# GpSimd in the text's order, scatters one a turn, shared rows behind the last count, and more buffers for the routed tiles

## The chip, the cores and the metric

The kernel runs on one core of a Trainium2 chip. The metric is the device time of one execution in microseconds (us). Its engines are called as in the profile: PE (matrix products; PEld is its weight load), DVE (vector), ACT (activations), POOL (GpSimd) and SP (which issues most DMAs). Each engine takes its instructions in the order in which they were put down, and an instruction that waits holds all that stand behind it on that engine. L12 is line 12 of the kernel before.

## The reference, cut to what matters

Four layers follow each other on x, of shape (4, 512, 128), each a cross attention to a context of 77 tokens and a feed-forward part:

```python
x = x + L0_xattn(ctx, ctx, layernorm(x));   x = x + L0_ffn(layernorm(x))
x = x + L1_xattn(layernorm(x), ctx, ctx);   x = x + L1_ffn(layernorm(x))
x = x + L2_xattn(layernorm(x), ctx, ctx);   x = x + L2_ffn(layernorm(x))
x = x + L3_xattn(layernorm(x), ctx, mask);  x = x + L3_ffn(layernorm(x))
```

Three of the feed-forward parts are mixtures of eight experts. The first sends each token to its two best experts, weighted, and adds a shared expert that sees all tokens:

```python
gates = sigmoid(xf @ Wg);  vals, idx = top_k(gates, 2);  vals = vals / vals.sum(-1)
w = zeros.at[arange(T)[:, None], idx].add(vals)
shared = silu(xf @ Ws1) * (xf @ Ws3) @ Ws2
h = silu(einsum('td,edf->tef', xf, We1)) * einsum('td,edf->tef', xf, We3)
out = (shared + einsum('tef,efd,te->td', h, We2, w)) / 3
```

The second sends each token to one expert, up to a capacity of 320 tokens per expert, with one hidden layer of 512; the fourth sends each token to one expert without a capacity. The third feed-forward part is dense.

## The kernel before

The 2048 tokens are worked on in four rows of 512 (the batch entries, b = 0 to 3). A row is 128 partitions by NT = 4 blocks of 128 features.

**Routing.** After a row's first attention, `route0` (L1064) normalises it: statistics `mv` on DVE, `std` and `rstd` on POOL (L192, L194), the result `xr` on DVE (L199). It transposes it (L207), copies it to `hT` (L213), forms the gates (L1027, L1036), and picks two experts per token on DVE. `Router.count` (L922, last product L943) counts on PE how many earlier tokens go to each expert, so each token has a place `to` (L1106) in a buffer `xbuf` in DRAM. `Router.send` (L956) then scatters the rows there with indirect DMAs that POOL issues (L958): four for the first choice, then a copy of `xr` on POOL (L1099), then four for the second. After the last row `Router.tiles` (L975) forms on DVE a table `tab` of the buffer positions and experts of the tiles (256 places of one expert each), and `far`, which marks empty places. The second layer's `route1` (L1296) copies the tokens beside the normalised rows on POOL (`xw`, L1300) and has four scatters a row. The last layer's goes as the first's, with four.

**Routed tiles.** The first feed-forward part (from here: the first stage, 217 to 322 us) has 23 tiles. `tile_rows` (L1041) lets SP read a position and an expert from `tab` and issue two loads: the rows `xt` (L1046, three buffers) and the expert's weights `wt` (L1049, four buffers). `layer1` (L1248 on) transposes the rows on PE, copies them to `hTt` on ACT, takes the tokens' numbers `idx` on DVE (L1252) and their weights `wgt` (L1254), both in three buffers, and `gated` (L1213) forms the hidden layer in two halves: products L1218 and L1219 on PE, silu on ACT (L1221), product `hid` on DVE (L1222). `layer2` multiplies by the second weights (L1262), scales to `ye` on ACT (L1268, three buffers), and `give_rows` (L1052) scatters `ye` to the tokens' places in `ybuf` by two indirect DMAs on POOL (L1053). A buffer of `idx` or `ye` is free again when its scatter has read it. The second part (middle stage, 471 to 526 us) has eight tiles, one per expert; the last (1021 to 1114 us) has 15 tiles with products L1370 and L1381, `idx` at L1744, and `ye` at L1754 on DVE, scattered to the output.

**The shared expert and the next constants.** `shared(b)` (L1226) uses `gated` on a whole row (L1218, L1219, L1221, L1222), multiplies by the second weights (L1231) and adds to x on DVE (L1236). Rows 0 and 1 stand in the text ahead of the tiles, rows 2 and 3 behind them. `PlainCross` (L1110) forms the keys and values of the second attention from the context: a product L1117, and `values3` (L235), which fills three tiles with zeros on POOL (L240) and has twelve products L245 whose results DVE adds a bias to and spreads out (L248, L257).

**What sets the order.** Outside of the attentions a scheduler puts each engine's instructions in the order of its own costs; it may move an instruction ahead of others of the text as far as its data allow. Inside `attend` (L505) the order of the text is kept for the engines of ORDERED (L501: PE, DVE and ACT), not for POOL, and what stands behind in the text may be placed between them by the scheduler. There the text itself interleaves generators: `side` is the list of those that are open, `turn` (L481) steps the one that is due, a `yield` ends its turn, and `yield -1` asks for the next turn. When the main sequence is over, `round_of_turns` steps each in turn, with two warming products between rounds (`warm`, L166, a product of constants whose result nobody reads).

Of the kernel before, what the change touches and what calls it, by code (L numbers as in the profile page):

```python
# [8 lines left out]
F32 = mybir.dt.float32  # L9
BF16 = mybir.dt.bfloat16  # L10
U8 = mybir.dt.uint8
I32 = mybir.dt.int32  # L12
# [47 lines left out]
def tile_kernel(ctx: ExitStack, tc: tile.TileContext, ins, out):  # L60
# [438 lines left out]
                side_step(gen)  # L499

    ORDERED = {getattr(mybir.EngineType, e) for e in ("PE", "DVE", "Activation")}  # L501

    def attend(units, lead, turns, fill=8):

# [37 lines left out]
                if begun and (u < 3 or ends[u - 3] - 1 <= n):  # L542
                    launch(u)

        with tc.manual_schedule(engines=ORDERED):
            pairs = 0
            launch(0)
            while starts[0] in side:
                warm(fill)
                side_step(starts[0])  # L550
                turn()
            for n in range(-lead, len(seq) + 1):
                un = old = None
                if 0 <= n < len(seq):
                    u, i = seq[n]
                    if i == 0:
                        side_drain(readies[u])
                    if i < units[u].shape.steps:
                        un = units[u]
                if 0 < n:  # L560
                    v, j = seq[n - 1]
                    if j < units[v].shape.steps:
                        old = units[v]
                        if j == 0 and old.late is not None:
                            if v not in lates:
                                lates[v] = old.late(old)
                                side_add(lates[v])
                            side_drain(lates[v])
                whole = n + lead >= len(seq)
                if whole:  # L570
                    banks[:] = [3]
                for k in range(2):
                    if un is not None and (k == 0 or not whole):
                        sc = []
                        for c in (0, 1) if whole else (k,):
                            sc.append(un.scores_t(i, c, whole and pairs % 3 == 2))
                            pairs += whole
# [336 lines left out]
    class Router:  # L914
# [7 lines left out]
        def count(self, b, oh):  # L922
# [17 lines left out]
                    pp[:, :n], lhsT=onesb, rhs=runb.rearrange("p i e -> p (i e)"), start=False, stop=False  # L940
                )
            for i in range(1, NT):
                nc.tensor.matmul(  # L943
                    pp[:, i * E : n], lhsT=onesb, rhs=of[:, : (NT - i) * E], start=False, stop=i == NT - 1
                )
            return pp[:, :n].rearrange("p (i e) -> p i e", e=E)
# [8 lines left out]

        def send(self, rows, to):  # L956
            for i in range(NT):
                d = nc.gpsimd.indirect_dma_start(  # L958
                    out=self.xbuf, out_offset=bass.IndirectOffsetOnAxis(ap=to[:, i : i + 1], axis=0),
                    in_=rows[:, i, :], in_offset=None, bounds_check=self.xbuf.shape[0] - 1, oob_is_err=False,  # L960
                )
                apart(d, self.sent)
                self.sent.append(d)
# [76 lines left out]

    def tile_rows(pool, tab, xbuf, w, t, width, wcols, sent):  # L1041

        xt = pool.tile([128, 2 * width], F32, tag="xt", name="xt", bufs=3)
        at = nc.sync.value_load(tab[0:1, 0, t : t + 1], min_val=0, max_val=xbuf.shape[0] - TS)
        src = xbuf[bass.ds(at, TS), :].rearrange("(p two) d -> p (two d)", two=2)
        after_all(nc.sync.dma_start(out=xt, in_=src), sent)  # L1046
        wt = pool.tile([128, wcols], F32, tag="wt", name="wt", bufs=4)
        e = nc.sync.value_load(tab[0:1, 1, t : t + 1], min_val=0, max_val=(E - 1) * 128)
        nc.sync.dma_start(out=wt, in_=w[bass.ds(e, 128), :])  # L1049
        return xt.rearrange("p (i d) -> p i d", i=2), wt  # L1050
# [14 lines left out]
    def route0(b):  # L1065
# [28 lines left out]
        for k, (oh, m) in enumerate(((oh1, m1), (oh2, m2))):  # L1094
# [9 lines left out]
            slot = router0.pick(at, oh, "slot")  # L1104
            to = small.tile([128, NT], I32, tag="to", name="to")
            nc.vector.tensor_scalar(to, slot, -1.0, None, ALU.add)  # L1106
            router0.send(rows, to)


    class PlainCross:  # L1110
# [95 lines left out]

    mid, ahead = ExitStack(), ExitStack()
    ap1 = ahead.enter_context(tc.tile_pool(name="ahead", bufs=2))
    plain = PlainCross(ap1, NK, p2, p2("kb"), p1("bv1"))
    with tc.tile_pool(name="moe0", bufs=2) as mpool:  # L1210
        tab, far = router0.tiles(N0)

# [22 lines left out]
            xf = xs[b].rearrange("p i d -> p (i d)")  # L1235
            nc.vector.scalar_tensor_tensor(xf, py, 1.0 / 3.0, xf, ALU.mult, ALU.add)  # L1236

        for b in range(2):
            shared(b)
        warm(16)  # L1240
        given = []
        first = {}

        def layer1(t):
# [3 lines left out]
                nc.tensor.transpose(ps[:, i * 128 : (i + 1) * 128], xt[:, i, :D], ident)  # L1248
            hT = mpool.tile([128, TS], F32, tag="hTt", name="hTt")
            nc.scalar.copy(hT, ps[:, :TS])  # L1250
            idx = mpool.tile([128, 2], I32, tag="idx", name="idx", bufs=3)
            nc.vector.tensor_tensor(idx, xt[:, :, 129], far[:, t, :], ALU.max)  # L1252
            wgt = mpool.tile([128, 2], F32, tag="wgt", name="wgt", bufs=3)
            nc.vector.tensor_copy(wgt, xt[:, :, 128])  # L1254
            first[t] = gated(hT, w[:, 0:256], w[:, 256:512], TS), w, idx, wgt

        def layer2(t):
            hid, w, idx, wgt = first.pop(t)
            py = mm_tile()
            for i in range(2):  # L1260
                for c in range(2):
# [1 line left out]
                        py[:, i * 128 : (i + 1) * 128], lhsT=hid[:, c, i * 128 : (i + 1) * 128],  # L1263
                        rhs=w[:, 512 + c * 128 : 640 + c * 128], start=c == 0, stop=c == 1,
                    )
            ye = mpool.tile([128, 2, D], F32, tag="ye", name="ye", bufs=3)
            for i in range(2):
                nc.scalar.mul(ye[:, i, :], py[:, i * 128 : (i + 1) * 128], wgt[:, i : i + 1])  # L1268
            for i in range(2):
# [27 lines left out]
    def route1(b):  # L1297
# [23 lines left out]
        nc.vector.tensor_tensor(far, far, pos, ALU.add)  # L1321
        to = small.tile([128, NT], I32, tag="to", name="to")
        nc.vector.tensor_tensor(to, far, first, ALU.add)
        router1.send(xr, to)

    def finish1(b, o_tok):
        yield from project_add(o_tok, 1, p2("wo"), xs[b])
# [60 lines left out]
    with tc.tile_pool(name="moe1", bufs=2) as mpool:  # L1388
# [10 lines left out]
        def layer1(e):  # L1399
# [11 lines left out]
                nc.tensor.transpose(ps[:, o : o + n], xe[:n, i, :D], ident[:n, :n])  # L1411
            hT = mpool.tile([128, CAP], F32, tag="hTe", name="hTe")
            nc.scalar.copy(hT, ps[:, :CAP])
            idx = mpool.tile([128, 3], I32, tag="idx", name="idx", bufs=3)
            nc.vector.tensor_tensor(idx[:, 0:2], xe[:, 0:2, 257], far1[:, e, 0:2], ALU.max)
            nc.vector.tensor_tensor(idx[:64, 2:3], xe[:64, 2, 257:258], far1[:64, e, 2:3], ALU.max)
            held[e] = xe, idx, relu_layer1(mpool, hT, p3("w1")[:, e * 512 :], p3("b1")[:, e * 4 :], CAP)
# [1 line left out]
        def layer2(e):  # L1419
# [2 lines left out]
            pt = mm_tile()  # L1422
            for i, (o, n) in enumerate(cuts):
                nc.tensor.transpose(pt[:n, i * D : (i + 1) * D], yT[:, o : o + n], ident)
            ye = mpool.tile([128, 3, D], F32, tag="ye", name="ye", bufs=3)
# [26 lines left out]
    def route3(b):  # L1452
# [17 lines left out]
        router3.send(xr, to)  # L1470


    ys = {}
# [256 lines left out]
    with tc.tile_pool(name="moe3", bufs=2) as mpool:  # L1730
# [5 lines left out]
        def layer1(t):  # L1736
# [6 lines left out]
            idx = mpool.tile([128, 2], I32, tag="idx", name="idx", bufs=3)  # L1743
            nc.vector.tensor_tensor(idx, xt[:, :, 256], far[:, t, :], ALU.max)  # L1744
            held[t] = xt, w, idx, relu_layer1(mpool, hT, w, w[:, 1024:1028], TS)

        def layer2(t):
# [5 lines left out]
            ye = mpool.tile([128, 2, D], F32, tag="ye", name="ye", bufs=3)  # L1753
            nc.vector.tensor_tensor(  # L1754
                ye, pt[:, :TS].rearrange("p (i d) -> p i d", i=2), xt[:, :, D : 2 * D], ALU.add
            )
# [136 lines left out]
```

## Time and profile before

| | us |
|---|---|
| median of 3 runs | 1118.06 (1117.11 to 1126.39) |
| the profiled execution | 1115.88 |
| its span, first to last instruction | 1114.0 |
| busy: PE / DVE / ACT / POOL | 913.8 / 551.7 / 428.6 / 293.4 |
| first attention and routing | 0 to 217 |
| first stage of routed tiles | 217 to 322 |
| second attention and routing | 338 to 470 |
| middle stage (eight experts) | 471 to 526 |
| third and fourth attention, dense part | 528 to 1016 |
| last stage of routed tiles | 1021 to 1114 |

The mean granted clock of PE is 0.886 of full speed. A row of a timeline gives the start, the duration, the engine, the line, what it made of what, and in brackets how long the engine had stood idle before it and what ended that. A row of waits gives who waited, for what, how long in total, how often, and the longest. "SPq" is the queue of DMA issues on SP. Not every instruction has its record in the trace (a few per cent are missing).

### The profile page before, as it was taken

Reading aid. Unit: us, or ns where it says so; the run is one execution under the profiler, and the core shown is the slowest. Engines: PE = TensorE matmul, PEld = TensorE weight load, DVE = VectorE, ACT = ScalarE, POOL = GpSimd, SP = SyncE. Lnnn points to the kernel's source line nnn. Section 1 sums busy time; section 2 is a strip of 40 time slices with the busy share of each in tenths; the row PEclk is TensorE's granted clock in tenths of the full one; section 3 lists DMA queues with packets and bytes.
Section 4 is the critical chain, followed back from the end, with each engine's and each line's share of the span. In section 5 each row is a group of like instructions: output and inputs, shape, how many; then the busy total and the mean of one; then the engine's idle time right before and its main releaser. Section 6 shows DMA issues by size and latency. Waiting matters only on the chain. (4 is left out here: it accounts for less than half of the span.)

```text
span 1114.0 us, 15855 instructions
## 1 busy us (share of the span) xinstructions
PE 913.8 (82%) x5602; PEld 448.8 (40%) x5602; DVE 551.7 (50%) x1733; ACT 428.6 (38%) x647; POOL 293.4 (26%) x350
## 2 busy tenths in 40 slices
PE   5898876587878987696699888888899999983885
PEld 2444433376753434254355234332222232331764
DVE  3455334422235655232655325468787888813232
ACT  1164332133421544032232143334565666760332
POOL 4010334234431222335422002324003101012233
PEclk8999688889997997699688589999899999996999
DMA  9999200155433000121200000773516200002552
GB/s 301 283 272 294 62 20 19 45 167 152 144 101 152 10 26 23 31 79 40 54 4 10 1 0 6 167 160 83 118 40 150 52 3 21 2 20 68 169 164 85
DMA packets 75393, 100.20 MB, mean 90 GB/s; under 512 B 9143, under 2 KB 63365, under 8 KB 74291
## 3 DMA queue, kind: packets, MB, share of 16 engines
q1 hardware_dynamic: 66915, 88.08, 29.5%
q0 software_dynamic: 5760, 9.33, 2.5%
q10 hardware_dynamic: 2640, 1.79, 0.5%
q8 instruction: 44, 0.72, 0.3%
q14 instruction: 34, 0.28, 0.1%
HBM read 49.69 MB, written 51.13 MB: 90 GB/s over the span
## 5 line engine op out<-in xcount | busy, mean ns | idle before, releaser
L393 ACT ACTIVATE pT<-sc 128x1024 f32<-128x1024 f32 (+5 forms) x198 | 201.3, 1022 | 174.6 <-PE sc L382 108.3
L838 DVE TENSOR_REDUCE mx<-mm 128x1 f32<-128x512 f32 x248 | 156.7, 682 | 38.1 <-PE mm L308 32.3
L407 PE MATMUL mm<-pT,vv 128*32 128x256 f32 (+4 forms) x1216 | 117.3, 454 | 4.6 <-ACT oT L426 3.7
L776 DVE TENSOR_REDUCE mx<-mm 128x4 f32<-128x308 f32 (+1 forms) x120 | 51.7, 472 | 83.9 <-PE mm L312 48.9
L1053 POOL DMA_INDIRECT ybuf<-ye,idx x70 | 67.5, 965 | 93.5 <-ACT ye L1268 50.3
L170 PE MATMUL mm<-steady,onesb 128*128 128x512 bf16 x222 | 66.4, 426 | 12.7 <-DVE vs L1177 1.7
L192 POOL TENSOR_SCALAR std<-mv 128x4 f32<-128x4 f32 x40 | 9.6, 239 | 243.0 <-DVE mv L190 228.1
L958 POOL DMA_INDIRECT xbuf<-xw,to x32 | 32.2, 1006 | 118.7 <-DVE to L1469 60.3
L373 PE MATMUL sc<-q,kbd 32*77 32x512 f32 (+2 forms) x204 | 57.8, 701 | 0.6 <-ACT pT L393 0.6
L213 ACT COPY hT<-mm 128x512 f32<-128x512 f32 x28 | 16.4, 584 | 106.4 <-PE mm L207 106.3
L382 PE MATMUL sc<-qr,kr 32*128 32x512 bf16 x246 | 48.3, 394 | 4.0 <-DMA qr<-mTS 4.0
L308 PE MATMUL mm<-eight 64*128 64x512 bf16 x184 | 44.8, 393 | 7.2 <-DVE mx L838 5.1
L958 POOL DMA_INDIRECT xbuf<-xr,to x32 | 32.1, 1002 | 57.2 <-DMA xbuf<-zero 18.3
L776 DVE TENSOR_REDUCE mx<-sc 128x8 f32<-128x616 f32 (+1 forms) x36 | 27.3, 797 | 39.0 <-PE sc L329 28.8
L407 PEld LDWEIGHTS mm<-pT,vv 128*32 128x32 f32 (+3 forms) x1216 | 26.5, 109 | 49.1 <-issue 39.4
L1053 POOL DMA_INDIRECT out_dram<-ye,idx x30 | 29.1, 971 | 57.4 <-DVE ye L1754 34.1
L1222 DVE TENSOR_TENSOR hid<-sc,sl 128x256 f32<-128x256 f32 (+1 forms) x54 | 24.7, 462 | 36.5 <-ACT sl L1221 30.3
L1218 PE MATMUL sc<-hTt,wt 128*128 128x256 f32 x92 | 32.4, 438 | 12.6 <-DVE hid L1222 4.4
L194 POOL TENSOR_TENSOR rstd<-std,power 128x4 f32<-128x4 f32 x40 | 41.6, 1041 | 3.3
L170 PEld LDWEIGHTS <-onesb 128*128 128x128 bf16 x222 | 22.2, 105 | 49.3 <-issue 35.1
L1221 ACT ACTIVATE sl<-sc 128x256 f32<-128x256 f32 (+1 forms) x54 | 22.3, 415 | 46.6 <-PE sc L1219 32.5
L382 PEld LDWEIGHTS <-kr 32*128 32x128 bf16 x256 | 11.5, 91 | 70.7 <-issue 70.7
(341 smaller groups left out, 1780.3 us busy)
## 6 DMA issues: line engine op xcount, KB each, us to landing
xbuf<-zero SPq DMA_DIRECT2D x25, 1040.0 KB
wt<-in_w_dram SPq DMA_DIRECT2D x23, 384.0 KB
wt<-in_w_dram SPq DMA_DIRECT2D x15, 514.5 KB
qkt<-tt SPq DMA_DIRECT2D x32, 192.0 KB
p<-in_p_dram SPq DMA_DIRECT2D x1, 4120.0 KB
xt<-xbuf SPq DMA_DIRECT2D x15, 257.0 KB
eight<-qkt SPq DMA_DIRECT2D x6, 512.0 KB
xt<-xbuf SPq DMA_DIRECT2D x23, 130.0 KB
```

What stands on the lines that cost most here:

```text
L170: nc.tensor.matmul(ps, lhsT=onesb, rhs=steady, start=True, stop=True)
L194: nc.gpsimd.tensor_tensor(rstd, std, power.to_broadcast([128, NT]), ALU.pow)
L308: nc.tensor.matmul(sc[:, cols], lhsT=lhs, rhs=rhs, start=True, stop=self.mk is None)
L373: nc.tensor.matmul(sc[g % 2][:n], lhsT=lhs, rhs=rhs, start=True, stop=False)
L382: nc.tensor.matmul(sc[g % 2][:n], lhsT=lhs, rhs=rhs, start=False, stop=self.mk is None)
L393: nc.scalar.activation(p[:n], both[:n], AF.Exp, scale=self.scale)
L407: nc.tensor.matmul(self.acc[32 * g : 32 * g + 32, cols], lhsT=self.shape.values(self, i, g), rhs=self.p[i, g // 2][:n, g % 2, cols], start ...
L776: nc.vector.tensor_reduce(un.mx.rearrange("p q (g r) -> p q g r", g=NG)[:, i, g, :], sc.rearrange("p g (r k) -> p g r k", k=self.nk), axis ...
L838: nc.vector.tensor_reduce(mx[:, i % 4, g, i // 4], sc, axis=AX.X, op=ALU.max, negate=True)
L958: d = nc.gpsimd.indirect_dma_start(out=self.xbuf, out_offset=bass.IndirectOffsetOnAxis(ap=to[:, i : i + 1], axis=0), in_=rows[:, i, :], in ...
L1053: d = nc.gpsimd.indirect_dma_start(out=out_rows, out_offset=bass.IndirectOffsetOnAxis(ap=idx, axis=0), in_=ye, in_offset=None, bounds_chec ...
L1218: nc.tensor.matmul(sc[:, 0, :n], lhsT=w1[:, cs], rhs=hT, start=True, stop=True)
```

## The change

Line numbers below 500 are the same in both kernels; behind that the new kernel's are one to three higher.

- In `attend` the text's order is kept for POOL too (the first two attentions use it; the third and fourth have their own loop, which stays as it is).
- `send` is a generator now: it ends its turn after each scatter while other generators are open.
- `shared(0)`, `shared(1)` and `PlainCross` are put down inside `tc.issue_after(router0.last.ins)`, behind the last product of the last row's count; before, the scheduler had spread their products over the ends of rows 2 and 3. The 16 warming products behind them are gone.
- Buffers: `xt` 3 to 5 (both stages that use it), `idx` and `wgt` 3 to 8, `ye` 3 to 6, in all three stages.

On POOL the new order is: row 2's `std` and `rstd` after five of row 1's eight scatters, row 3's after three of row 2's and the three memsets; in the second attention row 3's after two of four scatters, with the copy `xw` behind it. On PE the ends of rows 2 and 3 hold no shared-expert or constants' products; these follow the last count. On DVE the shared rows' `hid` and the constants' additions stand among the instructions that form `tab` and `far`, and the last of them behind the first tiles' `idx`. On SP a read of the table now stands between the loads of tile 0's rows and its weights. Arithmetic and the number of scatters are unchanged.

```diff
+    WITH_POOL = ORDERED | {mybir.EngineType.Pool}
...
-        with tc.manual_schedule(engines=ORDERED):
+        with tc.manual_schedule(engines=WITH_POOL):
...
-                nc.tensor.matmul(
+                self.last = nc.tensor.matmul(
                     pp[:, i * E : n], lhsT=onesb, rhs=of[:, : (NT - i) * E], start=False, stop=i == NT - 1
...
         def send(self, rows, to):
             for i in range(NT):
+                if i and len(side) > 1:
+                    yield -1
                 d = nc.gpsimd.indirect_dma_start(
...
-        xt = pool.tile([128, 2 * width], F32, tag="xt", name="xt", bufs=3)
+        xt = pool.tile([128, 2 * width], F32, tag="xt", name="xt", bufs=5)
...
-            router0.send(rows, to)
+            yield from router0.send(rows, to)
...
-    plain = PlainCross(ap1, NK, p2, p2("kb"), p1("bv1"))
...
-        for b in range(2):
-            shared(b)
-        warm(16)
+        with tc.issue_after(router0.last.ins):
+            for b in range(2):
+                shared(b)
+            plain = PlainCross(ap1, NK, p2, p2("kb"), p1("bv1"))
...
-            idx = mpool.tile([128, 2], I32, tag="idx", name="idx", bufs=3)
+            idx = mpool.tile([128, 2], I32, tag="idx", name="idx", bufs=8)
...
-            wgt = mpool.tile([128, 2], F32, tag="wgt", name="wgt", bufs=3)
+            wgt = mpool.tile([128, 2], F32, tag="wgt", name="wgt", bufs=8)
...
-            ye = mpool.tile([128, 2, D], F32, tag="ye", name="ye", bufs=3)
+            ye = mpool.tile([128, 2, D], F32, tag="ye", name="ye", bufs=6)
...
```

The same two lines for `idx` (3 to 8) and `ye` (3 to 6) follow in the middle and the last stage, and `yield from` at the other two calls of `send`.

More of the change, by code (lines that the diff above doesn't have):

```diff
@@ L1323, in route1 @@
         nc.vector.tensor_tensor(to, far, first, ALU.add)
-        router1.send(xr, to)
+        yield from router1.send(xr, to)
     def finish1(b, o_tok):
@@ L1413, in layer1 @@
             nc.scalar.copy(hT, ps[:, :CAP])
-            idx = mpool.tile([128, 3], I32, tag="idx", name="idx", bufs=3)
+            idx = mpool.tile([128, 3], I32, tag="idx", name="idx", bufs=8)
             nc.vector.tensor_tensor(idx[:, 0:2], xe[:, 0:2, 257], far1[:, e, 0:2], ALU.max)
@@ L1424, in layer2 @@
                 nc.tensor.transpose(pt[:n, i * D : (i + 1) * D], yT[:, o : o + n], ident)
-            ye = mpool.tile([128, 3, D], F32, tag="ye", name="ye", bufs=3)
+            ye = mpool.tile([128, 3, D], F32, tag="ye", name="ye", bufs=6)
             for i, (o, n) in enumerate(cuts):
@@ L1469, in route3 @@
         nc.vector.tensor_scalar(to, slot, -1.0, None, ALU.add)
-        router3.send(xr, to)
+        yield from router3.send(xr, to)
     ys = {}
@@ L1742, in layer1 @@
             nc.scalar.activation(hT, ps[:, :TS], AF.Identity, bias=p7("be2"), scale=p7("g2"))
-            idx = mpool.tile([128, 2], I32, tag="idx", name="idx", bufs=3)
+            idx = mpool.tile([128, 2], I32, tag="idx", name="idx", bufs=8)
             nc.vector.tensor_tensor(idx, xt[:, :, 256], far[:, t, :], ALU.max)
@@ L1752, in layer2 @@
                 nc.tensor.transpose(pt[:, i * 128 : (i + 1) * 128], yT[:, i * 128 : (i + 1) * 128], ident)
-            ye = mpool.tile([128, 2, D], F32, tag="ye", name="ye", bufs=3)
+            ye = mpool.tile([128, 2, D], F32, tag="ye", name="ye", bufs=6)
             nc.vector.tensor_tensor(
```

## Prediction

> **What bounds the kernel now.** The engine table has PE busy for 82% of 1114.0 us, an average over stages with different limits, so I went on to single stages: the two stages of routed tiles and the ends of the first two attentions, each by its waits, then its timeline. The waits from 217 to 330 us (first routed stage; waiter, line, releaser, us in total, times, longest):
>
> ```profile
> POOL ybuf L1053 <- ACT ye L1268: 50.3, 14, 14.0
> DVE idx L1252 <- DMA ybuf<-ye,idx: 24.0, 13, 3.5
> ```
>
> GpSimd's 50.3 us is slack: a tile has two scatters of 0.97 + 0.30 us, 2.55 in all. The 24.0 us matters. `idx` has three buffers, so tile t's indices wait until tile t-3's scatter has landed, and DVE, in order, holds the `hid` products behind them. Timelines of DVE and PE (start, us, engine, line):
>
> ```profile
> 237.29 0.16 DVE L1252 TENSOR_TENSOR idx<-xt,far 128x2 int32<-128x2 f32 x1 [0.58 <-DMA ybuf<-ye,idx]
> 240.10 0.43 DVE L1222 TENSOR_TENSOR hid<-sc,sl 128x256 f32<-128x256 f32 x1 [2.66 <-ACT sl L1221]
> 240.39 0.70 PE L1218 MATMUL sc<-hTt,wt 128*128 128x256 f32 x2 [2.92 <-ACT hTt L1250]
> ```
>
> The reader sees the pipeline run dry: with the indices late, PE stands for 2.92 us. Windows (busy us and count of PE, PEld, DVE, ACT, POOL; then granted clock, DMA share, GB/s):
>
> ```profile
> 215.00:220.00 5.00, 0.00 (x0) 0.00 (x0) 0.00 (x0) 0.00 (x0) 1.81 (x2) 0.50 0.12 40
> 240.00:245.00 5.00, 4.61 (x17) 4.04 (x18) 1.39 (x4) 1.99 (x7) 0.00 (x0) 0.66 0.31 100
> 223.00:314.00 91.00, 74.08 (x391) 63.49 (x392) 24.31 (x88) 36.44 (x108) 40.77 (x42) 0.92 0.50 149
> 294.90:305.50 10.60, 9.39 (x55) 8.04 (x56) 3.08 (x13) 4.47 (x14) 5.83 (x6) 1.00 0.63 182
> ```
>
> Tile 0's first product starts at 223.01, tile 22's at 313.88: 22 periods of 4.13 us, 90.9 in all. The last row holds three tiles that hardly waited: (10.57 - one stall of 1.21) / 3 = 3.12 us, all of it PE at full clock. The waits of the last stage, 1021 to 1114 (the second from SP's own queue):
>
> ```profile
> DVE idx L1744 <- DMA out_dram<-ye,idx: 30.5, 12, 3.8
> SPq L1046 <- DVE ye L1754: 37.4, 11, 5.4
> ```
>
> The same, and `xt`, three buffers too, keeps its load back until `ye` of three tiles before. First layers start at 1034.91 (tile 1) to 1099.62 (tile 14): 13 periods of 4.98 us, against 4.05 to 4.48 where none waited.
>
> The end of the first attention, on GpSimd, then PE:
>
> ```profile
> 189.34 0.97 POOL L958 DMA_INDIRECT xbuf<-xr,to  x1 [0.30 <-issue]
> 190.30 1.02 POOL L240 MEMSET vv<- 128x512 f32 x2
> 191.37 0.12 POOL L264 MEMSET vv<- 77x16 f32 x1
> 191.45 0.23 POOL L192 TENSOR_SCALAR std<-mv 128x4 f32<-128x4 f32 x1
> ```
> ```profile
> 165.35 1.49 PE L245 MATMUL mm<-p,ctx 128*115 128x128 f32 x6
> 166.63 1.92 PE L1218 MATMUL sc<-hT,p 128*128 128x512 f32 x2
> 171.34 1.03 PE L1027 MATMUL mm<-hT,p 128*8 128x512 f32 x2
> ```
>
> Row 3's `mv` was done at 186.38, but its `rstd` stood behind row 2's eight scatters and the memsets of the next constants: 5.07 us. Row 2's `rstd` likewise stood 5.5 us behind row 1's scatters. In row 2's tail the gate product L1027 ran at 171.34 though its operand was there by 166.2 (the copy of `hT` began at 165.60), behind shared-expert and constants' products.
>
> **GpSimd's order and the moved products.** All times are of the profiled execution. Row 2: in the new order its `rstd` stands behind five of row 1's eight scatters and a copy (0.61), so about 3.25 us earlier (three scatters of 1.275, less the copy); with the fill gone its tail is 2.5 shorter (10.26 us from `rstd` to the gate against 7.2 in row 3). So `mv` of row 3 comes at about 180.6. Its `rstd` now stands behind three of row 2's scatters and the memsets: `to` at 173.2 + 3.8 + 1.6 = 178.6, no longer late. So `rstd` 191.45 -> 180.65, **-10.8**. The other five scatters (6.4 us) go behind it, and end by 188.5, well ahead of row 3's own at about 196. Row 3's tail: two shared products on DVE (0.68 + 0.69) leave it, -1.4; colder products cost +0.6 (the second attention's tail, which has no fill, takes 7.8 us for the stretch that takes 7.2 here); the copy of `xr` now stands between the two groups of four scatters, +0.6. ACT's table load of 1.28 us there, which goes, ran beside the products up to the gate and gives nothing. So the load of tile 0 is issued at about 208.2 instead of 219.19, **-11.0**.
>
> The products moved are some 16.7 us of PE work at the durations they had; they begin after the last count (about 194) where 16 warming matmuls (3.61 us) and four L245 stood. What covers them is the gap until tile 0's rows land at about 210.3, 16.2 us long. What is left behind it: DVE takes tile 0's `idx` ahead of the last `hid` of shared row 1, seven L1231 products of it (1.1 us) stand ahead of tile 0's first product, behind tile 1's transposes, whose load waits a table read longer (+0.8). So first product 3.3 us after the landing instead of 1.68: 213.6 against 223.01, and four L245 right behind it, 1.1. **Net -8.3**; without that cover up to 3.3 more would be lost (-5), with it whole -10.
>
> **Buffers.** In the built order `idx` first waits for a scatter at the ninth tile and `ye` at the seventh. First stage: 22 x 3.12 = 68.6, plus 2.5 for the cold start that stays (first product pair 1.06 us against 0.59 until 228), plus 1.9 for some stalls: 73, **-17.9**. Bounds: 71.1 (-19.8), and 3.8 a tile, 83.6 (-7.3), if half the wait comes back elsewhere. At 3.12 the scatters still fit (2.55), two row loads and weight loads come at 514 KB a tile, and the 182 GB/s row has that pace. What the clock adds is a matter of rows: after the stall of 2.92 us it is 0.50 from 242 to 244. The Trainium skill ("TensorE: Matmul & The Clock Gate", Part 1: The HAM clock gate) has the clock halved only after an idle window of about 3.4 us. By that rule no stall of this stage would reach it, and the gain would be PE's idle time alone, 91.0 - 74.1 = 16.9 us; the trace disagrees, the clock fell, and the sum keeps to the rows.
>
> Last stage: 13 x (4.98 - 4.3) = **-8.8**; 4.3 lies between the unblocked 4.05 and 4.48, because weights still have four buffers and take 4.9 us to land. Bounds -12.1 (4.05) and -3.6 (4.7). The middle stage's tiles (eight experts) are PE-bound at 5.5 us, its `idx` waits off the path: nothing, at most -0.5.
>
> **Second attention.** Row 3's `mv` is done at 448.19; `rstd` runs at 451.88 behind four scatters and the copy `xw`. It now comes after two, at 448.9: **-3.0** (bounds -1.5 and -3.5). The two later attentions keep their order, so nothing from 528 to 1016 us moves but its start.
>
> **Sum.** -8.3 - 17.9 - 3.0 - 8.8 = -38.0. The profiled execution took 1115.88 us, 2.2 under the median of 1118.06: on the median's basis **1080 us**.
>
> **Rivals.**
> *Another wait takes over.* The weights keep four buffers, and SP waited 8.6 us for L1262 in the first stage already; if that, or the load's landing, holds the tiles at their old pace, only the attentions' gain is left: -8.3 - 3.0, **1107**. Against it: the 3.12 us stretch ran with the same four. Chance 0.08.
> *The front's gain is lost*: the moved 16.7 us run on a cold clock (0.50 at 215 to 220), tile 0 starts no earlier. For it: PE has little else there; against: products themselves warm the clock within 5 us (0.50, 0.71, then 1.00 from 220 on). 1080 + 8.3 = **1088**. Chance 0.17.
> *Slower: the clock stays at half in the first stage.* The place is the row of 23 tiles, now entered without the 16 warming matmuls, and with dry spells the clock would never come back. Each tile is 3.12 / 0.5 = 6.24 us, 22 of them 137.3, +46.4; less 8.3 + 3.0 + 8.8 it is **1144**. It decides from 4.13 + 20.1 / 22 = 5.04 us a tile, a mean clock of 0.62. Against: 0.92 in the stage before, with all its stalls. The page's section "HAM oscillation" tells of such a kernel, cold in each tile between waits for loads; no row here shows a clock that stays down. Chance 0.03.
> *It does not do what it says*: some other release of waits keeps `idx` and `rstd` as late as they were, **1118**. Against: the built order. Chance 0.03.
> *Better:* no stalls left, last stage at 4.05, front whole: -10 - 19.8 - 3.5 - 12.1, **1073**. Chance 0.09. The forecast keeps 0.60.
>
> **Range.** All lower bounds together give -5 - 7.3 - 1.5 - 3.6 = -17.4, 1101; below, the best case 1073 less what the 3.12 us may still hold of waits, taken as 0.3 a tile (6.6): 1066. So 1066 to 1101; outside are 1107, 1118 and 1144, 14 in 100. About 1% (11 us) is what a measurement of this kernel can tell from no change: faster by more, the forecast, the front's rival, the better case and some of the first rival (its 1107 lies on the bound), 0.91; within, the rest of that and the last rival, 0.06; slower, 0.03.
>
> **What would show it.** In the profile after: row 3's `rstd` at about 181, tile 0's rows issued at about 208; `idx` waits for the scatter near zero in both stages; periods near 3.3 and 4.3; the clock near 1.00 in the first stage. It would be wrong if DVE or SP stood for something new in the tiles, or if shared products still ran after 214.

## Result and profile after

| | before | changed |
|---|---|---|
| median of 4 runs | 1119.11 us (1117.11 to 1126.39) | 1075.67 us (1073.59 to 1084.02) |
| ratio, 95% interval | | 0.9601 (0.9533 to 0.9668) |
| the profiled execution | 1115.88 us | 1084.02 us |
| granted clock, mean | 0.886 | 0.893 |

The change made the kernel 4.0% faster; 1080 (1066 to 1101) was forecast. The profiled execution of the changed kernel is the slowest of its four, so a second one was taken below (1073.12 us).

Waits of the changed kernel from 210 to 300 us, the first stage of routed tiles (waiter, line, releaser, us in total, times, longest):

```profile
POOL ybuf L1056 <- ACT ye L1271: 45.9, 16, 17.7
DVE hid L1224 <- ACT sl L1223: 40.2, 31, 3.0
DVE idx L1255 <- DMA xt<-xbuf: 11.2, 8, 3.4
```

No wait for a scatter is left on `idx` (24.0 us before). What `idx` waits for now is its own rows. The waits of the last stage, 985 to 1083 us, and those of SP's queue from 990 on:

```profile
ACT hid L884 <- PE sc L1373: 29.8, 30, 3.4
...
DVE idx L1747 <- DMA xt<-xbuf: 17.4, 8, 5.4
```
```profile
SPq L1052 <- ACT yT L1388: 11.2, 6, 4.0
SPq L1049 <- DVE ye L1757: 3.8, 5, 1.5
```

ACT now waits for PE, and SP's wait for `ye` fell from 37.4 to 3.8 us. Windows (us, busy and count of PE, PEld, DVE, ACT, POOL, clock, DMA share, GB/s): the first stage from tile 0's first product to tile 22's, the last from tile 1's to tile 14's, and the last 3.5 us ahead of tile 0's first product:

```profile
216.49:298.03 81.54, 70.12 (x395) 60.86 (x395) 23.86 (x89) 34.80 (x105) 38.85 (x40) 0.96 0.50 156
1014.49:1067.49 53.00, 53.00 (x261) 42.95 (x260) 18.84 (x51) 24.38 (x52) 23.29 (x24) 1.00 0.60 187
213.00:216.50 3.50, 3.45 (x17) 3.48 (x18) 1.33 (x4) 0.37 (x1) 0.00 (x0) 0.50 0.85 238
```

The last stage is PE and nothing else: 53.00 of 53.00 us, 4.08 a tile. The first went from 90.9 to 81.5 us and still has PE idle for 11.4. The end of the first attention, on POOL and on PE:

```profile
178.39 1.01 POOL L240 MEMSET vv<- 128x512 f32 x2
179.46 0.12 POOL L264 MEMSET vv<- 77x16 f32 x1
181.04 0.27 POOL L192 TENSOR_SCALAR std<-mv 128x4 f32<-128x4 f32 x1 [1.46 <-DVE mv L190]
181.39 1.04 POOL L194 TENSOR_TENSOR rstd<-std,power 128x4 f32<-128x4 f32 x1
```
```profile
210.25 0.44 PE L1251 MATMUL mm<-p,xt 128*128 128x128 f32 x2 [1.73 <-DMA xt<-xbuf]
213.05 0.66 PE L1251 MATMUL mm<-p,xt 128*128 128x128 f32 x2 [2.36 <-DMA xt<-xbuf]
213.50 3.19 PE L1233 MATMUL mm<-p,hid 128*128 128x128 f32 x14
216.49 1.06 PE L1220 MATMUL sc<-hTt,wt 128*128 128x256 f32 x2
```

Row 3's `std` now waits for DVE's statistics, no longer for scatters. Tile 0's rows are there at 210.25, but its first product comes 6.2 us later: tile 1's transposes wait for their own rows until 213.05, and behind them seven products of shared row 1 take 3.19 us at half clock (0.50 in the window).

### The profile page after: what moved, and what is told of

It reads as the page before. It is cut to its first block, busy times and chain, and to the rows that moved or that the text cites. A ratio compares the mean times of both kernels' runs of the same rounds, so it can differ in the third digit from the quotient of the medians.

```text
span 1082.2 us, 15771 instructions
## 1 busy us (share of the span) xinstructions
PE 905.4 (84%) x5569; PEld 444.7 (41%) x5586; DVE 555.0 (51%) x1733; ACT 424.6 (39%) x645; POOL 293.7 (27%) x350
## 5 line engine op out<-in xcount | busy, mean ns | idle before, releaser
L407 PE MATMUL mm<-pT,vv 128*32 128x256 f32 (+4 forms) x1216 | 119.7, 463 | 4.7 <-ACT oT L426 3.8
L170 PE MATMUL mm<-steady,onesb 128*128 128x512 bf16 x189 | 61.3, 442 | 15.8 <-issue 1.9
L407 PEld LDWEIGHTS mm<-pT,vv 128*32 128x32 f32 (+3 forms) x1216 | 26.6, 110 | 49.5 <-issue 39.7
L207 PE MATMUL mm<-p,xhat 128*128 128x128 f32 x96 | 21.5, 337 | 24.1 <-DVE xhat L199 23.3
L382 PEld LDWEIGHTS <-kr 32*128 32x128 bf16 x256 | 11.4, 91 | 69.6 <-issue 69.6
L308 PE MATMUL mm<-kbd,q 32*128 32x154 f32 (+1 forms) x248 | 39.4, 377 | 0.0
```

The source lines that it names most:

```text
L170: nc.tensor.matmul(ps, lhsT=onesb, rhs=steady, start=True, stop=True)
L308: nc.tensor.matmul(sc[:, cols], lhsT=lhs, rhs=rhs, start=True, stop=self.mk is None)
L382: nc.tensor.matmul(sc[g % 2][:n], lhsT=lhs, rhs=rhs, start=False, stop=self.mk is None)
L407: nc.tensor.matmul(self.acc[32 * g : 32 * g + 32, cols], lhsT=self.shape.values(self, i, g), rhs=self.p[i, g // 2][:n, g % 2, cols], start ...
```

## Experiments

Each ratio is against the kernel before on the same chip, with its 95% interval; the median of before there was 1122.87 us for the first four, 1116.24 for the next four, and 1095.04 for three that ran on another chip. The stage columns are from the one profiled execution of each: from row 1's `std` to tile 0's first product ("front"), from there to tile 22's first product (first stage), and from tile 1's to tile 14's first product in the last stage.

| run | front | first stage | last stage | ratio |
|---|---|---|---|---|
| before | 92.0 | 90.9 | 64.7 | 1 |
| changed | 85.1 | 81.5 | 53.0 | 0.9601 (0.9533 to 0.9668) |
| changed, again | 84.0 | 73.5 | 53.0 | 0.9518 (0.9439 to 0.9596) |
| buffers alone | 91.6 | 96.9 | 53.0 | 0.9872 (0.9794 to 0.9950) |
| no buffers | 83.7 | 91.6 | 65.0 | 0.9878 (0.9805 to 0.9950) |
| GpSimd's order alone | 82.9 | 101.5 | 64.6 | 0.9960 (0.9901 to 1.0018) |
| changed, old GpSimd order | 91.6 | 73.5 | 53.0 | 0.9760 (0.9698 to 0.9822) |
| before, idx late | 90.9 | 94.6 | 64.6 | 1.0026 (0.9977 to 1.0074) |
| changed, idx late | 83.9 | 73.7 | 53.0 | 0.9697 (0.9635 to 0.9759) |
| same, more hTt and wt | 82.2 | 77.1 | 53.0 | 0.9688 (0.9605 to 0.9771) |
| changed, warming kept (other chip) | 88.3 | 66.7 | 53.0 | 0.9704 (0.9621 to 0.9787) |
| shared rows and buffers (other chip) | 88.8 | 68.5 | 53.0 | 0.9806 (0.9750 to 0.9862) |
| changed, only idx deep (other chip) | 85.7 | 68.6 | 57.7 | 0.9647 (0.9547 to 0.9747) |

**Buffers alone.** The kernel before with the new numbers (idx and ye in all three stages).

```diff
-        xt = pool.tile([128, 2 * width], F32, tag="xt", name="xt", bufs=3)
+        xt = pool.tile([128, 2 * width], F32, tag="xt", name="xt", bufs=5)
-            idx = mpool.tile([128, 2], I32, tag="idx", name="idx", bufs=3)
+            idx = mpool.tile([128, 2], I32, tag="idx", name="idx", bufs=8)
-            wgt = mpool.tile([128, 2], F32, tag="wgt", name="wgt", bufs=3)
+            wgt = mpool.tile([128, 2], F32, tag="wgt", name="wgt", bufs=8)
-            ye = mpool.tile([128, 2, D], F32, tag="ye", name="ye", bufs=3)
+            ye = mpool.tile([128, 2, D], F32, tag="ye", name="ye", bufs=6)
```

> The kernel before with the new numbers of buffers alone (xt 5, idx and wgt 8, ye 6). Theory A, each part of the change pays for itself: the two stages of routed tiles gain what they gained in the whole change, 90.9 to about 82 us from the first product of tile 0 to that of tile 22 (-9) and 64.7 to about 53 from tile 1 to tile 14 of the last stage (-11.7), the attentions nothing: 1119 - 21 = 1098. Theory B, the tiles ran faster for entering with other order and clock and not for the buffers: the first stage stays near 90, the last one alone gains: 1107.

Ratio 0.9872. The last stage has its whole gain (53.0 us), the first none, though `idx` waits for no scatter any more. Theory B's time fits (0.9872 x 1119 = 1105, for 1107), theory A's does not. Two readings of this profile: SP's waits from 212 to 316 us, then PE, SP and ACT together:

```profile
SPq L1049 <- PE mm L1262: 29.8, 8, 8.7
```
```profile
226.76 1.06 PE L1262 MATMUL mm<-wt,hid 128*128 128x128 f32 x8
...
229.80 0.33 SPq L1049 DMA_DIRECT2D wt<-in_w_dram  x1
229.81 0.62 ACT L1268 ACTIVATE ye<-mm,wgt 128x128 f32<-128x128 f32 x2 [2.18 <-issue]
...
232.21 0.80 PE L1262 MATMUL mm<-wt,hid 128*128 128x128 f32 x2 [2.31 <-DVE hid L1222]
```

PE's row has tile 2's products done at 227.82. Both instructions that wait for the last of them, tile 2's `ye` on ACT and the load of tile 6's weights into the same buffer on SP, go at 229.80, 2 us later. For the two tiles before, the same load went 0.1 us or less behind PE's row. The silu and `hid` behind them are late in turn, and PE stops. The loads that SP holds back are not what stops it: PE waits for weights once in the stage, 1.4 us at tile 0. Such stops of 1.6 to 3.7 us on L1262 stand in nearly every group of three tiles here, and the clock follows (0.85 over the stage). Ends of products are modelled in this profile, so it can't be read whether PE was late itself or its signals were. The engines that wait may be late themselves: SP came to its load only at 229.04 by its own records, and its register instructions are slow at times on this chip (last section).

**GpSimd's order and the moved rows, without the buffers.** On the changed kernel, in all three stages:

```diff
-        xt = pool.tile([128, 2 * width], F32, tag="xt", name="xt", bufs=5)
+        xt = pool.tile([128, 2 * width], F32, tag="xt", name="xt", bufs=3)
-            idx = mpool.tile([128, 2], I32, tag="idx", name="idx", bufs=8)
+            idx = mpool.tile([128, 2], I32, tag="idx", name="idx", bufs=3)
-            wgt = mpool.tile([128, 2], F32, tag="wgt", name="wgt", bufs=8)
+            wgt = mpool.tile([128, 2], F32, tag="wgt", name="wgt", bufs=3)
-            ye = mpool.tile([128, 2, D], F32, tag="ye", name="ye", bufs=6)
+            ye = mpool.tile([128, 2, D], F32, tag="ye", name="ye", bufs=3)
```

> The changed kernel with xt, idx, wgt and ye back at three buffers, so GpSimd's order, the scatters one a turn and the moved shared rows alone. Theory A: tile 0's first product near 216.5 (-6.5), the second attention -3, some 2.5 between, the stages at their old pace: about 1119 - 12 = 1107. Theory B: the first stage keeps much of its gain without the buffers: 1098.

Ratio 0.9878, the time that theory A gave (1105 for 1107). The front has all of its gain, both stages their old pace, and `idx` its old wait. Waits from 211 to 303 us:

```profile
DVE idx L1255 <- DMA ybuf<-ye,idx: 26.0, 15, 3.0
```

Alone, the two halves of the change give 1.3% and 1.2%; together they gave 4.0 and 4.8%. The rest is in the first stage: 90.9 before, 96.9 with the one half, 91.6 with the other, 81.5 and 73.5 with both. These are one or two profiles each.

**GpSimd's order alone.** On the kernel before, with the turns in all three calls of send:

```diff
-        with tc.manual_schedule(engines=ORDERED):
+        with tc.manual_schedule(engines=WITH_POOL):
...
+                if i and len(side) > 1:
+                    yield -1
```

> The kernel before with GpSimd in the text's order and the scatters one a turn alone; shared rows, constants, warming products and buffers as before. Theory A (the scatters ahead of rstd were most of the delay): row 3's rstd from 191.45 to about 183, tile 0's load near 211, first product near 214, since nothing cold stands ahead of it here, the second attention -3: 1119 - 12 = 1107. Theory C (the products in the rows' ends carry the gain, the scatters are hidden behind them once they are one a turn): row 3's rstd no earlier than 188, 1115.

Row 3's `std` stands at 180.84, with row 1's at 130.83 (before: 191.45 and 131.05), so the front has its whole gain without moving the shared rows, as theory A said. Its time of 1107 did not come: over ten runs the ratio is 0.996, nothing that can be told from no change. The first stage took 101.5 us in the profiled execution. By that profile the rows arrive earlier, and the tiles' stage gives it back.

```profile
178.42 0.12 POOL L264 MEMSET vv<- 77x16 f32 x1
180.84 0.27 POOL L192 TENSOR_SCALAR std<-mv 128x4 f32<-128x4 f32 x1 [2.30 <-DVE mv L190]
```

**The changed kernel again.** No edit.

> The changed kernel once more, for a second profile and for the spread of its runs (1069.6 to 1084.0 so far, the profiled one the slowest). If the spread has its place in one stage, the two profiles differ there: theory A has it in the first stage of tiles, whose pattern was broken by one long stop near 280 us; then tile 22's first product comes 4 to 10 us earlier than 81.5 us after tile 0's, with the rest alike. Otherwise the difference is spread over all stages.

Median 1072.89 us, profiled 1073.12. The first stage took 73.5 instead of 81.5 us, which is most of the 10.9 us between the two executions; a second part is the start (row 1's `std` at 127.73 instead of 131.40). The 8 us lie where theory A put them: the first profile has three stops of PE late in the stage, 1.63 us at 270.28, 2.96 at 281.71 and 1.73 at 295.53, and half clock until 219 and again for 3.4 us behind the longest; here no stop is above 1.05 us and the clock is 1.00 throughout. At the stop of 2.96 the silu starts at 280.82, over 2 us behind PE's row of its product (done at 278.5), as in the run with the buffers alone; so the changed kernel is not free of such stops. Windows of the first stage in this profile and in that of the run with the buffers alone:

```profile
211.72:285.26 73.54, 67.28 (x396) 58.78 (x395) 23.49 (x88) 34.03 (x104) 38.84 (x40) 1.00 0.54 172
```
```profile
216.38:313.30 96.92, 78.74 (x391) 67.77 (x391) 22.64 (x88) 35.90 (x108) 39.31 (x41) 0.85 0.43 138
```

**The changed kernel with GpSimd's old order.** The moved rows and the buffers stay.

```diff
-        with tc.manual_schedule(engines=WITH_POOL):
+        with tc.manual_schedule(engines=ORDERED):
...
-                if i and len(side) > 1:
-                    yield -1
```

> The changed kernel without GpSimd's order and without the turns between scatters: the moved shared rows and the new buffers stay. The buffers alone left the first stage where it was (96.9 us from tile 0's first product to tile 22's), the whole change brought 81.5 and 73.5. Theory A: what the buffers need is the start that the moved rows give (tile 1 transposed ahead of tile 0's products), so the first stage takes 73 to 82 here too, the last stage 53, only row 3's rstd is late again: 1119 - 9 - 9 to 17 - 12 + 9 = 1095 to 1100 with the rows' ends as before. Theory B: it needs GpSimd's order; the first stage stays above 90: 1107.

Ratio 0.976, 1092 on the base of 1119, and the first stage is at 73.5 us: theory A. By this profile the buffers pay in that stage once the shared rows are moved, and need no new order on GpSimd for it. What moved is three things at once (shared rows, constants, warming products gone); which of them it is, is not shown on this chip. The order's own worth on top of the rest is seen in the front, 91.6 against 84.0 to 85.1 us. The ratios give 1.6% (0.9601 against 0.976), but against different medians of before; the 7 us of the front and the 2.3 of the second attention are 0.8%.

**idx behind its tile's hid.** In layer1 of the first stage, with hids the list of gated's products on DVE:

```diff
-            first[t] = gated(hT, w[:, 0:256], w[:, 256:512], TS), w, idx, wgt
+            hid = gated(hT, w[:, 0:256], w[:, 256:512], TS)
+            with tc.issue_after(hids[-1].ins):
...
+            first[t] = hid, w, idx, wgt
```

On the kernel before:

> The kernel before with one thing changed in the first stage: idx and wgt of a tile are put behind that tile's last hid on DVE, with three buffers as before. Theory A (the wait that the prediction named: idx stands ahead of hid products and holds them until an old scatter has landed): idx now has its whole tile's time before it blocks anything, the first stage falls from 90.9 to 75 to 82 us, 1119 - 12 = 1107. Theory B (other stops hold the tiles, as in the run with the buffers alone, 96.9): no gain in that stage, 1119.

Ratio 1.0026, first stage 94.6 us: theory B. No wait of `idx` for a scatter is left (24.0 us before), and the kernel gains nothing. The edit has a price: `wgt` is read out of `xt` later, so SP holds the next rows' loads longer, 36.6 us in all from 216 to 316 (13.2 before, for `idx` and `wgt`).

```profile
SPq L1046 <- DVE wgt L1258: 36.6, 19, 6.2
```

But PE waits for no rows behind tile 0, so this is not what holds the tiles. Its seven long stops behind tile 0 are of 2.0 to 3.1 us, six of them ahead of L1266 (L1262 in the kernel before), as in the run with the buffers alone. On the changed kernel:

> The changed kernel with idx and wgt of a tile behind its last hid on DVE in the first stage. In the changed kernel idx of a tile stands up to three tiles ahead of the hid products and waits for that tile's rows (11.2 us in eight waits in one profile, 6.0 in five in the other). Theory A: these waits are the difference between the two profiles of the same kernel (81.5 and 73.5 us); here the stage takes 73 every time: 1072. Theory B: they are beside the path, the stop of 1.0 us in every third tile (ACT's copy hTt waits for a buffer, the silu stands behind it) and some stops of ACT set the pace: 73 to 82 as before, 1075.

73.7 us, and 0.9697: no better than the changed kernel. This profile has the stage that theory A gave, but so has one of the changed kernel; it is not shown that the waits of `idx` for its rows make the difference between the two.

**More buffers of hTt and wt on top.**

```diff
-            hT = mpool.tile([128, TS], F32, tag="hTt", name="hTt")
+            hT = mpool.tile([128, TS], F32, tag="hTt", name="hTt", bufs=4)
...
-        wt = pool.tile([128, wcols], F32, tag="wt", name="wt", bufs=4)
+        wt = pool.tile([128, wcols], F32, tag="wt", name="wt", bufs=6)
```

> The same, with four buffers of hTt instead of two (both stages of 256-row tiles) and six of wt instead of four. Theory A: the stop of 1.0 us in every third tile goes with the buffer, 10.3 us for three tiles become 9.4, the first stage 67 to 71: 1069. Theory B: PE's products are not what binds, the stop only moves to the next wait in DVE's or SP's order: 73 or more, 1074.

77.1 us and 0.9688: theory B. The stop of 1.0 us in every third tile stays, so neither buffer makes it.

**Warming products kept.** On the changed kernel:

```diff
             plain = PlainCross(ap1, NK, p2, p2("kb"), p1("bv1"))
+        warm(16)
```

> The changed kernel with the 16 warming products put back behind the moved rows. The scheduler then lets tiles 0, 1 and 2 be transposed before the first product, and from tile 3 on PE's order is that of the kernel before (the pair of transposes that stand together falls on tiles 4 and 5, 7 and 8 and so on, in the changed kernel on 3 and 4, 6 and 7). Theory A: this place of the pair is what holds the tiles of the first stage (96.9 and 94.6 us with the old place, whatever buffers or place idx had; 73.5 to 81.5 with the new one): the stage takes 90 or more, 1091. Theory B: the old place does no harm, what held the tiles was the cold start of tile 0 behind an idle PE: the stage takes 73 to 82, 1076.

**Shared rows moved alone, with the buffers.** On the kernel with the buffers alone:

```diff
-        for b in range(2):
-            shared(b)
-        warm(16)
+        with tc.issue_after(router0.last.ins):
+            for b in range(2):
+                shared(b)
```

> The kernel before with the new buffers, shared rows 0 and 1 behind the last count, no warming products; the next constants stay where they were, and GpSimd's order is the old one. PE's order in the first stage is the old one (pair on tiles 4 and 5), though tile 0 starts behind a PE that was busy. Theory A (place of the pair): the stage takes 90 or more, 1107. Theory B (start): 73 to 82, 1093.

**Only idx and wgt deep.** On the changed kernel, ye in all three stages:

```diff
-        xt = pool.tile([128, 2 * width], F32, tag="xt", name="xt", bufs=5)
+        xt = pool.tile([128, 2 * width], F32, tag="xt", name="xt", bufs=3)
-            ye = mpool.tile([128, 2, D], F32, tag="ye", name="ye", bufs=6)
+            ye = mpool.tile([128, 2, D], F32, tag="ye", name="ye", bufs=3)
```

> The changed kernel with xt and ye back at three buffers, idx and wgt at eight. Theory A: in the first stage idx was what waited, xt and ye hold little of it there: first stage 73.5 to 82 us; in the last stage xt holds the load back until ye of three tiles before, so it stays near its old 64.7 us: 1076 + 11 = 1087. Theory C: ye is the next that waits for a scatter (it did for nothing before, 0 us, because idx did it first), the first stage keeps 85 to 91: 1097.

These three ran on the other chip, where the kernel before takes 1095 us. The first stage took 66.7, 68.5 and 68.6 us, whatever the place of the pair, so theory A of the first two did not hold there. Theory B's time fits the second (0.9806 is 1097 on the base of 1119, for 1093), but not the first (0.9704 is 1086, for 1076). Windows of the stage in the three, in this order:

```profile
216.88:283.62 66.74, 65.39 (x386) 57.12 (x387) 22.58 (x80) 36.38 (x108) 39.32 (x41) 1.00 0.55 180
```
```profile
216.02:284.52 68.50, 68.25 (x404) 60.03 (x404) 24.61 (x89) 36.53 (x108) 39.32 (x41) 0.98 0.63 198
```
```profile
212.07:280.70 68.63, 67.29 (x395) 58.65 (x395) 24.40 (x89) 35.72 (x105) 38.84 (x40) 0.99 0.57 184
986.56:1044.26 57.70, 54.24 (x264) 43.47 (x264) 18.94 (x52) 25.51 (x52) 23.27 (x24) 1.00 0.58 183
```

PE is busy all but 0.3 to 1.4 us: 3.0 to 3.1 us a tile, the floor that the prediction took from its unblocked stretch. In none of the three is there a stop above 1.2 us. Whether the kernel on the chip of the first eight runs would lose its stops with the warming products or with the constants in their old place, or with `idx` alone deep, is not shown.

The last run is theory A's in the first stage: with `idx` alone deep it has all that the three reach. In the last stage theory A saw no gain, and 7.0 of the 11.7 us came (57.7, between 64.7 on the other chip and 53.0); the rest is missing because there `xt` still waits. SP's wait for `ye` is 28.4 us from 985 to 1062:

```profile
SPq L1049 <- DVE ye L1757: 28.4, 12, 4.6
```

Its ratio, 0.9647, is that of the whole change within the intervals.

**The kernel before again.** No edit.

> The kernel before once more, for a second profile. It has 90.9 us for the first stage in its one profile; with the new numbers of buffers it had 96.9, with the changed rows as well 73.5 to 81.5 on the same chip, and the last three runs, on another chip on which the kernel before itself took 1095 us, had 66.7 to 68.5 with no stop above 1.2 us. Theory D: the stops of 2 to 4 us in PE, ACT and SP of which no engine's row shows a cause belong to the chip, not to the kernel; then on the chip of 1095 us this kernel's first stage takes near 76 us (18 less than 94), with idx still waiting some 24 us in all, and on the chip of 1119 us near 91 again. Theory E: the stage differs between executions on one chip as much as that; then it is not near 91 on the chip of 1119 us, or not near 76 on the other.

Ratio of the kernel with itself 0.9994 (0.9945 to 1.0043), median 1119.26 us, on the chip of the first eight runs. Its profiled execution, of 1133.12 us, is the longest of its ten, so its stages are not compared and it tells neither theory from the other. What the kernel before has in its first stage on the other chip was not measured. An estimate: the last three runs gained 28, 21 and 33 us over it there; less what they would have gained in front, second attention and last stage by the first chip's profiles, 6 to 17 us are left for that stage, which puts it at 75 to 86 us. That leans to theory D, and shows nothing.

No version here beats the changed kernel beyond the intervals.

## Why the prediction was right, and where it was not

The time, the sign and the place were right: 1075.67 in 1066 to 1101, 1080 forecast, and the gain came from the four places named. But the largest term rests on a mechanism that alone gives nothing on this chip. By its steps, against both profiles of the changed kernel:

- **Front, -8.3.** Measured -6.9 and -8.0. The step on row 3's `rstd` is right nearly to the us (181.04, forecast 180.65; row 2's 159.06, forecast 158.9; tile 0's load 208.12, forecast 208.2). One cause in it is wrong: "the fill gone" was counted with 2.5 us in row 2's tail. GpSimd's order alone, with the fill in place, brings row 3's `std` to 50.0 us behind row 1's, the changed kernel to 49.6 and 50.4. The fill is hidden once `rstd` comes early; it costs (57.1 against 60.4 us) only in the old order. And the front of GpSimd's order alone is 82.9 us, better than the changed kernel's 85.1 and 84.0, since the moved products stand ahead of tile 0 there. The step gave 3.3 us from landing to the first product; it is 6.2 (5.9 in the second profile). The term mis-sized is the seven products of shared row 1, put at 1.1 us and measured at 3.19 (2.82 in the second): 1.1 is less than they take even at full clock (fourteen rows, where eight of L1262 take 1.06 us, so some 1.8, an estimate), and the clock was 0.50 (0.56 in the second). Another us is tile 1's rows: its transposes start 2.8 us behind tile 0's. The rival "the front's gain is lost" had this cold clock right, but the whole overrun is 2.9 us (2.6 in the second), not the gain. Its row "1.00 from 220 on" is misread: in windows of 5 us the clock before was 0.50 to 225, 0.71 to 230 and 1.00 from 230.
- **First stage, -17.9.** Measured -9.3 (81.5) and -17.3 (73.5). The forecast, 73 us, is what the better execution has. But the mechanism was too simple, and that the term came out is in part luck. The wait of `idx` for the scatter was there, and deep `idx` buffers took it away; that alone is not enough. With the buffers and the old order of rows, and with `idx` out of `hid`'s way, the stage gained nothing (96.9 and 94.6, on the chip where the changed kernel had 73.5). The prediction priced the buffers by themselves and gave the moved rows no part in this stage; they have one. The prediction's exhibit, PE's stop of 2.92 us at 240.39, was read as late indices; its own row names ACT's `hTt` as the releaser, and `idx` was done at 237.45, 2.65 us before `hid` went. What held `hid` was the silu, which started only at 239.69 although PE's rows have its product done at 236.02. In the same stretch SP took 0.70 us each for two register instructions whose records name no wait (at 237.48 and 238.20, rows below). That stop is of the kind seen in the run with the buffers alone, where work is taken up 2 us behind PE's rows. Why the moved rows rid that chip of most of them, and why the other chip had none, is open.
- **Second attention, -3.0.** Row 2's `std` to row 3's: 18.86 us before, 16.52 in both profiles after. So -2.3; the mechanism is the one named.
- **Last stage, -8.8.** Measured -11.7, near the outer bound of -12.1: 4.08 us a tile, PE-bound. The term mis-sized is the 4.3: weights in four buffers were thought to hold it. SP does wait for them (11.2 us), but early enough.
- **The middle stage, nothing.** 39.7 us from first to last scatter before, 39.8 and 39.1 after.

The rows of the kernel before at the stop of 2.92 us: ACT's silu, then SP's register instructions from 236 to 240 (line, engine, operation, count, shortest, median and longest in ns, first and last start):

```profile
239.69 0.38 ACT L1221 ACTIVATE sl<-sc 128x256 f32<-128x256 f32 x1 [3.44 <-remote]
```
```profile
L1048 SPq SEQ_ASSERT  x1: 700/700/700, 237.5 to 237.5; - x1
L1049 SPq FUSED_REGOPS  x1: 702/702/702, 238.2 to 238.2; - x1
```

The sum for the profiled execution was -38.0; it was -31.9 there, -42.8 in the second and -43.4 by the medians, so the forecast stands between its two profiles. Of the rivals, "another wait takes over" was true of the buffers by themselves (1105 by the ratio, for its 1107), and by stops of PE that no wait of PE for rows or weights explains. The slower rival, a clock that stays at half, did not come: 0.96 and 1.00 in the stage. The Trainium skill ("TensorE: Matmul & The Clock Gate", Part 1: The HAM clock gate) has the clock fall after an idle window of some 3.4 us. In the runs here stops of 1.0 us left it at 1.00 over the whole stage, and stops of 1.6 to 3.7 us brought it to 0.85; if PE was later than its rows, which is open, the idle time was longer than shown, and the rule may hold. The prediction's "the trace disagrees" was more than the rows bear out.

## What to carry to other kernels

Give the small results that an in-order engine hands to a slow scatter (here two columns of indices) as many buffers as tiles may be in flight: with the rest of the change in place, deep `idx` alone brought the whole first stage (68.6 us), while the last one needed deeper `xt` too (57.7 against 53.0). Put the short operation that the next row waits for (`rstd`) ahead of scatters on GpSimd's queue; with the rest of the change it moved tile 0's load 11 us ahead, but alone it brought no time (0.996): a gain at the entry of a stage is only kept if that stage isn't held by something of its own. Measure the parts together as well as alone: here 1.3% and 1.2% made 4%. And before a wait is called the cause, look whether the row of the stop names it: here it named another.

## What the runs showed of the hardware

The same program on another chip took 1095 us instead of 1116 to 1123, and there PE was busy for 98 to 99.6% of the first stage in the three kernels that ran. On the chip of the first eight runs, with the buffers alone, ACT and SP took up work 2 us behind the end that PE's rows show (227.82 against 229.80 and 229.81), on two engines at once. In that run ACT's `ye` starts 1.3 to 2.7 us behind the last L1262 row ahead of it in five of 23 tiles, ACT having stood idle, and 0.04 to 0.6 behind it in the others; in the three runs on the other chip it is 0.04 in every tile.

SP's records tell the two chips apart as well. FUSED_REGOPS is a register instruction that stands behind each read of the table, and its record names no semaphore that it waits for. Its median is 152 ns on both chips; on the chip of the first eight runs single ones take 0.7 us, on the other the longest takes 0.165. The rows of L1048, with the buffers alone, then with shared rows and buffers on the other chip (count, shortest, median and longest in ns):

```profile
L1048 SPq FUSED_REGOPS  x38: 3/152/724, 205.2 to 1073.4; - x38
```
```profile
L1048 SPq FUSED_REGOPS  x38: 147/152/165, 212.2 to 1035.7; - x38
```

Of SP's 306 register instructions (MOVE, FUSED_REGOPS, SEQ_ASSERT) 7 to 20 took more than 0.25 us in each of the eleven other profiles, that of the kernel before and both of the changed kernel included, and none in the three on the other chip (the longest 0.19). They don't all fall on a stop of PE. PE's stops above 1.3 us in the first stage, too, stand in those eleven alone, though not in all; but no kernel has a profile on both chips, and that the one brings about the other is not shown. None of this was expected, and its cause is open.

The length of a stop by PE's rows does not decide alone whether the clock falls: in the kernel before, 0.50 follows the stops of 2.92 us at 240.39 and 1.98 at 254.4 (windows 241.6 to 244.9 and 255.3 to 258.5), while behind stops of 1.82, 1.94 and 2.10 (at 267.3, 291.2 and 313.9) it stays at 1.00.
